# Chosen rows of an expert layer returned through DRAM, and layer 3's gate products moved to the end of an attention frame

## The chip, the cores and the metric

The kernel runs on one core of a Trainium2 chip. The metric is the device time of one execution in microseconds, as the median of several runs. The profile of one more execution shows where its time goes.

## The reference

The reference is a stack of eight sublayers on x of shape (8, 512, 128), each as `x = x + f(layernorm(x))`: four pairs of a token mixer and a feed-forward part. Three of them matter here.

```python
# layer 1's feed-forward part: 256 chosen rows get another value than the rest
x1 = einsum('btd,hd->bth', x, sw1) + sb1;  x2 = einsum('btd,hd->bth', x, sw2) + sb2
shared_out = einsum('bth,dh->btd', ln(silu(x1) * x2), sw3) + sb3
x_moe = x[index_b, index_t]                      # 256 rows
...                                              # gates, the best of 8 experts for each row
final_out = shared_out.at[index_b, index_t].set(shared_moe_out + expert_moe_out)

# layer 2's attention: 16 heads of 64 over 512 tokens, softmax over the query axis
scores = einsum('bhqp,bhkp->bhqk', q, k) / sqrt(64)
attn = softmax(scores, axis=2);  ctx = einsum('bhqk,bhkp->bqhp', attn, v)
out = concat(ctx) @ l_w.T + l_b

# layer 3's feed-forward part, with blockwise FP4 rounding of both sides
gate = fp4_linear(x, w_gate);  y = fp4_linear(x, w_up)     # 352 wide
out = fp4_linear(silu(gate) * y, w_down)
```

The indices are an input. In the data they name rows of the first two batches, but the kernel has to serve any.

## The kernel before

x lies in SBUF as eight blocks `x[b]` of 512 tokens (128 partitions, J = 4 tiles of 128). Every matmul is in float32; the profile counts each as two records. The order of instructions on every engine is the order in which the program calls them (`manual_schedule`), and each engine works its list in that order. Semaphore waits come from the tiles: a tile of a pool with n buffers waits until the tile n calls ago has been read.

Layer 0 and layer 1 come first. In layer 1, `stages` runs norms, linear attention and the shared part block by block; a written list of steps follows for the 256 chosen rows. `f_scale` writes each block's normed rows to the DRAM tile `by_rows` (SP's queue), `chosen_rows` gathers the 256 by two indirect transfers on GpSimd's queue (L968), and `chosen_out` leaves their new values in `val` (128 partitions, 2 rows each, 128 wide). `at_col` and `at_int` hold the rows' places, `rest` is 1 where a row is not chosen, and `inv` is one over how often it is.

To put `val` into x, the kernel makes a matrix `put` of zeros and ones for a block by comparing 0 to 511 with the places (`put_rows`, two DVE operations), multiplies it with `val` on TensorE (`put_product`: 8 matmuls, by way of `by_token`), and adds the product times `inv` (`scaled_add`, four DVE operations of L777). For block 0 this is at the end of layer 1 (`chosen_put`), before the norm of `x[0]`, its transposes and layer 2's first products. `keep_clock(n)` fills TensorE with products of the identity there. For blocks 1 to 7 it is in layer 2's frames 0 to 6 (`rows_in`).

`late` does layers 2 and 3 together. Layer 2's attention is cut into 64 frames n, one for a block and a pair of heads. A frame calls, in this order: `scores(n, 0)` (four products of q and k, the row maximum `nm` on DVE, four exponentials on ScalarE), with hook P between the exponentials of its two tiles; hook V; `context(n - 1)`; `weigh(n, 0)` (reciprocal on DVE, `vs` on GpSimd); hook G; `scores(n, 1)`; `queries(n + 2)` (q leaves PSUM by ScalarE, k by DVE); `output(n - 1)`; `values(n + 1)`; `weigh(n, 1)`; hook E. The steps of other layers are put into these hooks by `at(frame, hook, step)`. The PSUM banks are `two` (two buffers of two banks, for the scores), `c` and `o` (one each), and `one` with two buffers, which are given out in turn to queries (two), the gate products (two), each transpose and layer 3's convolution.

Layer 3 of block b follows by a plan of frames (`planned`), eight frames after that of the block before it: norm and a convolution of 20 taps (`conv_v` on DVE, `conv_s` on ScalarE and GpSimd, `conv_out` on TensorE), a second norm, FP4 rounding, four pairs of gate products `gated(j)` (two matmuls of 352 columns and a Tanh on ScalarE) with `gated_v(j)` on DVE, the rounding of h in two halves (`quant_h1`, `quant_h2`), its transposes (`turn_h(0)`, `turn_h(1)`) and the last product (`down`). Block 0's gate products are in frames 17 to 20, those of block 3 in frames 41 to 44, for example. Between frames 9 and 10 and between 17 and 18 layer 2's experts run for four blocks each.

Of the kernel before, what the change touches and what calls it, by code (L numbers as in the profile page):

```python
# [17 lines left out]
F32 = mybir.dt.float32  # L18
# [3 lines left out]
ALU = mybir.AluOpType  # L22
AX = mybir.AxisListType

P = 128
D = 128
NB = 8
TB = 512
# [132 lines left out]
def body(ctx, tc, dram, spans, x_in, ib, it, ic, ei, out):  # L161
# [527 lines left out]
    at_col = const.tile([P, 2], F32, tag="at_col", name="at_col")  # L689
    at_int = first.tile([P, 2], U32, tag="at_int", name="at_int")  # L690
    by_rows = tc.dram_tile([NT * P, D], F32, name="by_rows")
    inv = const.tile([P, NT], F32, tag="inv", name="inv")
    val = const.tile([P, 2, D], F32, tag="val", name="val")

# [78 lines left out]
    def scaled_add(b, pv, by):  # L773

        for j in range(J):
            t = b * J + j
            nc.vector.scalar_tensor_tensor(  # L777
                x[b][:, j, :], pv[:, j, :], by[:, t : t + 1], x[b][:, j, :], ALU.mult, ALU.add
            )

    def layer1():

# [5 lines left out]
        with tc.tile_pool(name="l1", bufs=2) as wp, tc.tile_pool(name="l1c", bufs=1) as once:  # L790
# [126 lines left out]
            def z_stats(b):  # L917
                t[b]["zby"] = stats_of(t[b]["z"], J)
# [178 lines left out]
            def chosen_out():  # L1097
# [25 lines left out]
                    val, val, po[:, : 2 * D].rearrange("p (m d) -> p m d", m=2), ALU.add  # L1123
                )

            def chosen_put():
                scaled_add(0, put_product(c_["put"]), inv)

# [22 lines left out]
            with tc.manual_schedule():  # L1151

                nc.scalar.activation(
                    stat.tile([P, J], F32, tag="nb", name="nb")[:, :1], half[:, :1], AF.Exp
                )
                for zt in zts:
                    nc.gpsimd.memset(zt[64:65, :], 1.0)
                for i in range(NB):
                    for f, lag in stages:
                        if 0 <= i + lag < NB and (f, i) != (turn_, 0):  # L1160
                            f(i + lag)


                gather(7)
                f_stats(5)
                output(6)
                z_scale(1)
                attend(7)
                f_scale(5)
                f_stats(6)  # L1170
                f_gate(2)
                turn_o(7)
                z_turn(1)
                output(7)
                f_stats(7)
                f_scale(6)
                chosen_biases()
                f_scale(7)
                z_out(1)
                z_stats(2)  # L1180
                chosen_rows()
                f_turn(5)
                f_gate(3)
                f_turn(6)
                z_stats(3)
                z_scale(2)
                f_gate(4)
                z_turn(2)
                f_turn(7)
                z_stats(4)  # L1190
                f_gate(5)
                z_out(2)
                z_stats(5)
                chosen_products()
                chosen_gates()
                z_scale(3)
                z_turn(3)
                chosen_select(0)
                f_product(6)
                z_out_by_three(3)  # L1200
                z_scale(4)
                z_turn(4)
                chosen_select(1)
                chosen_shared()
                chosen_norm()
                keep_clock(5)
                chosen_scale()
                z_out_by_three(4)
                t[6]["gated"]()
                z_stats(6)  # L1210
                f_product(7)
                chosen_mix()
                chosen_affine()
                keep_clock(8)
                chosen_turn()
                t[7]["gated"]()
                z_scale(5)
                c_["put"] = put_rows(0, wp, nc.vector)
                z_turn(5)
                chosen_out()  # L1220
                z_stats(7)
                z_scale(6)
                z_out_by_three(5)
                chosen_put()

                by = stats_of(x[0], J)
                z_turn(6)
                z_out_by_three(6)
                keep_clock(10)
                xn = norm.tile([P, J, D], F32, tag="xn", name="xn")  # L1230
                scaled(xn, x[0], by, J)
                nc.gpsimd.tensor_tensor(
                    x[0], x[0], bc["lb"].unsqueeze(1).to_broadcast([P, J, D]), ALU.add
                )
                keep_clock(6)
                t[0]["next"] = turned(norm, "xt", xn)
                z_scale(7)
                z_turn(7)
                z_out_by_three(7)
# [111 lines left out]
    def late():  # L1351
# [11 lines left out]
        with tc.tile_pool(name="a2", bufs=2) as wp, tc.tile_pool(name="l3", bufs=1) as lp:  # L1363
# [283 lines left out]
            def layer3(b, xp, tile_, part=(0, J), conv_bank="one", h_tag="h"):  # L1647
# [171 lines left out]
                stats2, scale2, _, t2 = norm_steps(b, None, None, part)  # L1819
                return SimpleNamespace(**{k: v for k, v in locals().items() if callable(v)})  # L1820

            def planned(b, f0_):

                s = layer3(b, *shared3(b))


                soon = b < 2 or b == NB - 2
                z = 9 - soon
                plan = [
                    (1, "V", s.stats) if b < 2 else (0, "E", s.stats),  # L1830
                    (1, "G", s.scale),
                    (1, "E", s.turn_),
                    (2, "V", lambda: s.conv_v(1, 2, 3, 4)),
                    (2, "G", lambda: s.conv_s(6, 7)),
                    (2, "E", lambda: s.conv_s(8, 9, 10)),
                    (2, "E", lambda: s.conv_v(5)),
                    (3, "G", lambda: s.conv_s(11, 12)),
                    (3, "E", lambda: s.conv_s(13, 14, 15)),
                    (4, "G", lambda: s.conv_s(16, 17)),
                    (4, "E", lambda: s.conv_s(18, 19, 20)),  # L1840
                    (5, "V", s.join),
                    (5, "E", s.conv_out),
                    (5, "E", s.stats2),
                    (6, "G", s.scale2),
                    (6, "E", s.quant_x1) if soon else (7, "V", s.quant_x1),
                    (z - 1, "V", s.quant_x2),
                    (z - 1, "E", s.turn_x),
                    (z + 2, "V", lambda: s.quant_h1(0)),
                    (z + 3, "V", lambda: s.quant_h2(0)),
                    (z + 4, "V", lambda: s.quant_h1(1)),  # L1850
                    (z + 5, "V", lambda: s.quant_h2(1)),
                    (z + 5, "P", lambda: s.turn_h(0)),
                    (z + 6, "P", lambda: s.turn_h(1)),
                    (z + 6, "E", s.down),
                ]
                for j in range(J):
                    plan.append((z + j, "P", lambda j=j: s.gated(j)))
                    plan.append((z + j, "V", lambda j=j: s.gated_v(j)))
                for frame, kind, f in plan:
                    at(f0_ + frame, kind, f)  # L1860
                return s
# [101 lines left out]
            def rows_in(b):  # L1963
                made = {}

                def make():
                    made["put"] = put_rows(b, lp, nc.vector, "cg")

                def product():
                    scaled_add(b, put_product(made["put"]), inv)  # L1970

                return make, product

            for b in range(1, NB):
                make, product = rows_in(b)
                at(b - 1, "V", make)
                at(b - 1, "E", product)

            with tc.manual_schedule():
                nc.vector.tensor_scalar(qb, a2["qb"], 0.125, None, ALU.mult)  # L1980
                fetch(0)
                xts[0] = t[0]["next"]
                queries(0)
                for n in range(N):
                    scores(n, 0, lambda: (n > 0 or (values(0), queries(1)), hook(n, "P")))
                    if n - 1 in experts_after:
                        waiting()
                    hook(n, "V")
                    if n - 1 in exs:
                        ct = context(n - 1)  # L1990
                    weigh(n, 0)
                    hook(n, "G")
                    scores(n, 1, lambda: None)
                    queries(n + 2)
                    if n > 0:
                        output(n - 1, ct)
                    values(n + 1)
                    weigh(n, 1)
                    hook(n, "E")
                    if n in experts_after:  # L2000
                        eb, made = experts_after[n]
                        kept = []
                        waiting = experts(eb, made["xt"], lambda: kept.append(context(n)))
                        ct = kept[0]
                end()
# [40 lines left out]
```

## Time and profile before

| | |
|---|---|
| median of 6 runs | 1521.85 us (1518.63 to 1525.66) |
| the profiled execution | 1515.39 us |
| its span | 1513.6 us, 22428 instructions |
| mean granted TensorE clock | 0.978 |
| frames 0 to 63 | begin at 552.81 us and 1428.92 us |
| exponentials of layer 2 | 512, 688 ns each (L1483) |
| products of the chosen rows | 128 records, 275 ns each (ps<-val,put) |
| DMA | 55.12 MB, mean 36 GB/s |

A profile line of the timeline gives the start in us from the span's start, the time from the first start to the last end of the group, then engine, line, operation, the tiles (out<-in), the shapes and the count; in brackets is the idle time before it and what ended it. Matmuls overlap in the records, so that a row of 16 of 275 ns takes less than 16 times that.

### The profile page before, as it was taken

To read this page: it belongs to the slowest core of one execution; us is meant where nothing else is said; L and a number is where in the kernel's file an instruction comes from. 1 tells how busy PE (TensorE), PEld (TensorE's weight loads), DVE (VectorE), ACT (ScalarE), POOL (GpSimd) and SP (SyncE) were. 2 spreads that over 40 slices of the span, in tenths; PEclk is the share of its full clock that TensorE was granted. 3 is DMA by queue.
4 is the path that set the end of the run, shared out by engine and by line. 5 is a ranking of instruction groups with operands and counts; after the bars stand their busy time and mean duration, and the time that the engine had idled before them with its cause. 6 is when DMAs were issued, how large, how long until landed. Compare 5 with 4: busy or idle time off the path is not lost.

```text
span 1513.6 us, 22428 instructions
## 1 busy us (share of the span) xinstructions
PE 1416.1 (94%) x7782; PEld 680.2 (45%) x7782; DVE 1031.7 (68%) x2129; ACT 1046.5 (69%) x2141; POOL 643.2 (42%) x742
## 2 busy tenths in 40 slices
PE   7789999998789889999999999999999999999975
PEld 3652222222366655543444444445445454454453
DVE  6776667767476636661664397786886877867857
ACT  6869999888776545564776486776776767767632
POOL 6647666665655321110441053352441623524432
PEclk9899999999999889999999999999999999999997
DMA  5049999977321010000100000000000000000000
GB/s 181 1 58 130 134 130 127 127 114 103 84 85 36 11 29 1 0 1 0 28 1 1 1 1 7 1 1 8 1 1 8 1 8 1 0 8 1 1 8 14
DMA packets 25443, 55.12 MB, mean 36 GB/s; under 512 B 5266, under 2 KB 18130, under 8 KB 20851
## 3 DMA queue, kind: packets, MB, share of 16 engines
q1 hardware_dynamic: 24688, 51.99, 20.4%
q10 hardware_dynamic: 578, 1.57, 0.3%
q8 instruction: 62, 1.02, 0.3%
q14 instruction: 51, 0.41, 0.1%
q0 software_dynamic: 64, 0.13, 0.0%
HBM read 47.35 MB, written 6.32 MB: 35 GB/s over the span
## 4 chain that ended last, share of the span: by engine, by line
PE 67%; ACT 13%; DVE 12%; DMA 4%; issue 2%; POOL 2%; SPq 0%; POOLq 0%; DVEq 0%; ACTq 0%
PE ps L247 65%; ACT hm L556 5%; DMA gs<-gates 3%; ACT ex L1483 2%; ACT hm L555 2%; DVE pr L568 1%; DVE nm L1477 1%; DMA gates<-eq 1%; POOL rs L244 1%; ACT xn L1399 1%; DVE fm L1284 1%; DVE s L702 1%; DVE frc L1267 1%; ACT xn L713 0%; DVE fa L1285 0%
## 5 line engine op out<-in xcount | busy, mean ns | idle before, releaser
L1483 ACT ACTIVATE ex<-ps,nm 128x512 f32<-128x512 f32 x512 | 345.8, 688 | 192.5 <-DVE nm L1477 192.5
L1477 DVE TENSOR_REDUCE nm<-ps 128x2 f32<-128x1024 f32 x256 | 300.4, 1215 | 48.3 <-PE ps L247 48.0
L247 PE MATMUL ps<-q,k 64*128 64x512 f32 x1024 | 258.4, 621 | 4.8 <-ACT ex L1483 4.0
L247 PE MATMUL ps<-ex,vs 128*64 128x512 f32 x1024 | 233.8, 598 | 0.0
L1498 POOL TENSOR_TENSOR vs<-v,sm 128x256 f32<-128x256 f32 x128 | 81.5, 637 | 337.5 <-DVE sm L1497 290.0
L574 POOL TENSOR_TENSOR acc<-acc,pr 128x512 f32<-128x512 f32 x119 | 166.6, 1400 | 107.6 <-DVE pr L568 102.9
L556 ACT ACTIVATE hm<-ps,blob_f 128x1536 f32<-128x1536 f32 x128 | 196.3, 1533 | 0.0
L247 PE MATMUL ps<-xt,blob_a 128*128 128x512 f32 x304 | 153.0, 630 | 0.1
L247 PE MATMUL ps<-h,w 32*128 32x512 f32 x1024 | 148.0, 639 | 3.6 <-DVE eq L467 1.9
L247 PE MATMUL ps<-hm,w 128*32 128x512 f32 x1024 | 136.4, 605 | 11.3 <-DVE pr L568 10.3
L247 PEld LDWEIGHTS ps<-q,k 64*128 64x128 f32 x1024 | 87.5, 186 | 131.1 <-issue 75.3
L568 DVE SCALAR_TENSOR_TENSOR pr<-ps,blob_f,gs 128x512 f32<-128x512 f32 x120 | 89.9, 749 | 74.5 <-PE ps L247 60.7
L1683 POOL TENSOR_TENSOR acs<-acs,prod 128x512 f32<-128x512 f32 (+1 forms) x104 | 130.0, 1250 | 14.3 <-ACT prod L1682 9.6
L247 PEld LDWEIGHTS ps<-ex,vs 128*64 128x64 f32 x1024 | 67.8, 136 | 144.5 <-issue 124.3
L243 POOL TENSOR_SCALAR rs<-mv 128x4 f32<-128x4 f32 (+1 forms) x69 | 17.7, 257 | 213.0 <-DVE mv L1389 146.4
L555 ACT ACTIVATE hm<-ps,blob_f 128x512 f32<-128x512 f32 x128 | 88.0, 687 | 29.0 <-PE ps L247 28.9
L1483 ACT ACTIVATION_READ_ACCUMULATOR ex<-ps,nm 128x1 f32 x512 | 105.6, 206 | 0.0
L247 PEld LDWEIGHTS ps<-xt,blob_a 128*128 128x128 f32 x304 | 53.2, 194 | 87.8 <-issue 60.5
L1445 DVE TENSOR_TENSOR v<-ps,blob_bc 128x512 f32<-128x512 f32 x64 | 44.2, 691 | 70.7 <-PE ps L247 44.2
L247 PEld LDWEIGHTS ps<-h,w 32*128 32x128 f32 x1024 | 40.9, 183 | 111.7 <-ACT hm L555 86.1
L247 PEld LDWEIGHTS ps<-blob_a,ct 128*128 128x128 f32 x512 | 67.0, 191 | 32.3 <-issue 29.2
L244 POOL TENSOR_TENSOR rs<-rs,half 128x4 f32<-128x4 f32 (+1 forms) x69 | 72.4, 1050 | 5.8
(292 smaller groups left out, 2265.6 us busy)
## 6 DMA issues: line engine op xcount, KB each, us to landing
gs<-gates SPq DMA_DIRECT2D x256, 128.0 KB
blob_f<-in_f SPq DMA_DIRECT2D x1, 2560.0 KB
blob_a<-in_a SPq DMA_DIRECT2D x1, 2056.0 KB
x<-in_x SPq DMA_DIRECT2D x8, 256.0 KB
gates<-eq SPq DMA_DIRECT2D x8, 256.0 KB
by_rows<-fxn SPq DMA_DIRECT2D x8, 256.0 KB
ge<-gates SPq DMA_DIRECT2D x4, 512.0 KB
out<-x SPq DMA_DIRECT2D x7, 256.0 KB
```

What stands on the lines that cost most here:

```text
L243: nc.gpsimd.tensor_scalar(t, var, EPS, None, ALU.add)
L244: nc.gpsimd.tensor_tensor(t, t, half[:, : t.shape[-1]], ALU.pow)
L247: nc.tensor.matmul(out_, lhs, rhs, start=start, stop=stop)
L555: nc.scalar.activation(hm[:, 0, :], p1, AF.Gelu, bias=bias)
L556: nc.scalar.activation(hm[:, 1:, :], p3, AF.Gelu, bias=bias)
L568: nc.vector.scalar_tensor_tensor(pr, po, f0["b2"][:, e : e + 1], gs, ALU.add, ALU.mult)
L574: nc.gpsimd.tensor_tensor(acc[:, b, :], acc[:, b, :], pr, ALU.add)
L1445: nc.vector.tensor_tensor(v, pv, bias, ALU.add)
L1477: nc.vector.tensor_reduce(nm, ps, AX.X, ALU.max, negate=True)
L1483: nc.scalar.activation(ex[kt][:, i, :], ps[:, i, :], AF.Exp, bias=nm[:, i : i + 1], accum_out=sm[:, kt, i : i + 1],)
L1498: nc.gpsimd.tensor_tensor(vs[:, tiles, :, :], vs_[n][:, tiles, :].rearrange("p j (i n) -> p j i n", i=2), sm[:, tiles, :].unsqueeze(3).to_ ...
L1683: nc.gpsimd.tensor_tensor(t["acs"], t["acs"], p, ALU.add)
```

## The change

It has two parts. The rows of blocks 1 to 7 no longer come by a product. At the start of layer 1, a cleared tile `nought` is written by SP's queue to blocks 1 to 7 of a new DRAM tile `back`. After `chosen_out`, `chosen_back` scatters `val` to its places in `back` by two indirect transfers on GpSimd's queue. In frames 0 to 6, hook V issues a read of one block of `back` on SP's queue into a tile "cg", and hook E adds it to `x[b]` on GpSimd. Block 0 stays with its product.

In layer 3, the gate products j = 1 to 3 of blocks 1 and up go from hook P of frame z + j to hook E of the same frame, behind `values(n + 1)`, and their `gated_v` goes from hook V of that frame to hook V of the next. In those frames (`early_q`) `queries(n + 2)` is called between the exponentials of `scores(n, 1)`, where it stood behind them. `turn_h(0)` goes from hook P to hook E of frame z + 5, for all blocks of the plan. z is 8 for blocks 0, 1 and 6 and 9 otherwise, counted from the block's first frame (9 for block 0, 17 for block 1, then 24, 32 and so on).

```diff
+    back = tc.dram_tile([NT * P, D], F32, name="back")
...
+            def chosen_back():
+                for m in range(2):
+                    nc.gpsimd.indirect_dma_start(
+                        back, bass.IndirectOffsetOnAxis(at_int[:, m : m + 1], 0), val[:, m, :], None
+                    )
...
                 for zt in zts:
                     nc.gpsimd.memset(zt[64:65, :], 1.0)
+                nought = once.tile([P, J, D], F32, tag="nought", name="nought")
+                nc.gpsimd.memset(nought, 0.0)
+                for b in range(1, NB):
+                    nc.sync.dma_start(
+                        back[b * TB : (b + 1) * TB, :].rearrange("(j p) d -> p j d", p=P), nought
+                    )
...
                 chosen_out()
+                chosen_back()
                 z_stats(7)
...
+            early_q = set()
...
+                for j in range(J):
+                    if b > 0 and j > 0:
+                        early_q.add(f0_ + z + j)
+                        plan.append((z + j, "E", lambda j=j: s.gated(j)))
+                        plan.append((z + j + 1, "V", lambda j=j: s.gated_v(j)))
+                    else:
+                        plan.append((z + j, "P", lambda j=j: s.gated(j)))
+                        plan.append((z + j, "V", lambda j=j: s.gated_v(j)))
...
-                    (z + 5, "P", lambda: s.turn_h(0)),
+                    (z + 5, "E", lambda: s.turn_h(0)),
                     (z + 6, "P", lambda: s.turn_h(1)),
                     (z + 6, "E", s.down),
-                for j in range(J):
-                    plan.append((z + j, "P", lambda j=j: s.gated(j)))
-                    plan.append((z + j, "V", lambda j=j: s.gated_v(j)))
...
-                def make():
-                    made["put"] = put_rows(b, lp, nc.vector, "cg")
-                def product():
-                    scaled_add(b, put_product(made["put"]), inv)
+                def fetch_rows():
+                    made["rows"] = lp.tile([P, 4, TB], F32, tag="cg", name="rows")[:, 0, :]
+                    nc.sync.dma_start(
+                        made["rows"].rearrange("p (j d) -> p j d", j=J),
+                        back[b * TB : (b + 1) * TB, :].rearrange("(j p) d -> p j d", p=P),
+                    )
+                def add():
+                    rows_ = made["rows"].rearrange("p (j d) -> p j d", j=J)
+                    nc.gpsimd.tensor_tensor(x[b], x[b], rows_, ALU.add)
...
-                    scores(n, 1, lambda: None)
-                    queries(n + 2)
+                    scores(n, 1, lambda: queries(n + 2) if n in early_q else None)
+                    if n not in early_q:
+                        queries(n + 2)
```

More of the change, by code (lines that the diff above doesn't have):

```diff
@@ L1847, in planned @@
                     (z - 1, "E", s.turn_x),
+                ]
+                for j in range(J):
[6 more added lines that the diff above has]
+                        plan.append((z + j, "V", lambda j=j: s.gated_v(j)))
+                plan += [
                     (z + 2, "V", lambda: s.quant_h1(0)),
@@ L1964, in rows_in @@
                 made = {}
-                def make():
-                    made["put"] = put_rows(b, lp, nc.vector, "cg")
-                def product():
-                    scaled_add(b, put_product(made["put"]), inv)
-                return make, product
+                def fetch_rows():
[7 more added lines that the diff above has]
+                    nc.gpsimd.tensor_tensor(x[b], x[b], rows_, ALU.add)
+                return fetch_rows, add
             for b in range(1, NB):
-                make, product = rows_in(b)
-                at(b - 1, "V", make)
-                at(b - 1, "E", product)
+                fetch_rows, add = rows_in(b)
+                at(b - 1, "V", fetch_rows)
+                at(b - 1, "E", add)
             with tc.manual_schedule():
```

## The prediction

> **What bounds the kernel now.** I read the page first: the busy line and the chain that ended last.
>
> ```profile
> PE 1416.1 (94%) x7782; PEld 680.2 (45%) x7782; DVE 1031.7 (68%) x2129; ACT 1046.5 (69%) x2141; POOL 643.2 (42%) x742
> ...
> PE 67%; ACT 13%; DVE 12%; DMA 4%; issue 2%; POOL 2%; SPq 0%; POOLq 0%; DVEq 0%; ACTq 0%
> ```
>
> TensorE is both the busiest engine and two thirds of the chain, so I asked for the stage that the diff touches, cut into frames. A frame runs from one frame's first score product (ps<-q,k) to the next. The columns are the stretch, its length, and busy time of PE, PEld, DVE, ACT and POOL, then the clock and DMA.
>
> ```profile
> 632.12:645.03 12.91, 12.91 (x70) 6.85 (x69) 9.31 (x23) 6.73 (x18) 2.70 (x5) 1.00 0.00 0
> 656.58:667.70 11.12, 11.12 (x53) 5.06 (x53) 6.75 (x9) 7.13 (x19) 1.23 (x2) 1.00 0.00 0
> ...
> 1189.82:1202.32 12.50, 12.50 (x58) 5.73 (x57) 11.41 (x14) 9.20 (x23) 8.92 (x8) 1.00 0.00 0
> ...
> 1215.22:1227.14 11.92, 11.92 (x59) 5.66 (x58) 11.24 (x29) 7.76 (x24) 6.31 (x8) 1.00 0.00 1
> ```
>
> These are frames 6, 8, 44 and 46. PE is busy for the whole of each. A bare frame (8) is 11.12 us; frame 6 adds one product of chosen rows, 44 one pair of gate products (1.38 us), 46 six transposes of h (0.80). So a frame is as long as its PE work, and two things follow. Work taken off PE shortens a frame by its full length; work moved inside a frame gains nothing, and loses if it must wait in the new place.
>
> **The rows: what leaves.** In frames 0 to 6 eight products (16 records) go from PE, and six DVE operations with them. The PE timeline of frame 4 ends so:
>
> ```profile
> 617.34 1.95 PE L247 MATMUL ps<-val,put 128*128 128x128 f32 x16
> 619.22 1.99 PE L247 MATMUL ps<-q,k 64*128 64x512 f32 x8
> ```
>
> From 617.34 to 619.22 is 1.88 with the 0.1 that any frame has at its end, so the product is worth 1.78 us, and 12.90 - 11.12 = 1.78 says the same. Nothing is late next: frames 8 and 13 are such frames without it and have no idle PE. In frame 0 the last exponential of the frame ends 12.70 us in, and the second score product of frame 1 asks for its bank at 13.4. Sum: 7 x 1.78 = 12.46 us off. The DVE operations (2 x 0.48 and 4 x 0.34 per block) were beside PE work and count as nothing.
>
> **The rows: what comes.** Per block one SP read of 256 KB and one POOL add of 128x512, 1.27 us by the row of L954. The add stands behind vs of its frame (ends about 12.8 us in), and the next vs that queues behind it is due at 5.6 in the frame after; the read is issued when the previous add frees its tile, about 3 us into the frame, and the indirect reads of before landed in 2.7 us. That leaves some 6 us; without that cover, vs and the context product behind it would be late by what is missing. I take 0.
>
> In layer 1, POOL clears one tile behind three clears of 0.52 us, before the first rs. SP's seven writes stand before by_rows, which is first issued 27 us later: 0. POOL's q and v operations follow, and PE waits for the v clear at 416.11, so I take 0.3 us; the bounds are 0 and 0.5.
>
> At the end of layer 1 the two scatters stand on POOL between val and the rs of z_stats(7). Their price is that of the two gathers, one engine and size (other direction, so between nothing and twice):
>
> ```profile
> 501.18 1.23 POOL L968 DMA_INDIRECT row<-by_rows,at_int  x1 [2.21 <-DMA by_rows<-fxn]
> 502.71 0.96 POOL L968 DMA_INDIRECT row<-by_rows,at_int  x1 [0.30 <-DVE s L898]
> ...
> 503.70 0.26 POOL L243 TENSOR_SCALAR rs<-mv 128x4 f32<-128x4 f32 x1
> ```
>
> The wait before the first ended at 500.35, so POOL is held 3.35 us. val is done at 534.48: POOL is free at 537.85 where the rs of z_stats(7) now starts at 535.37. Behind it queue that norm's three operations (1.65 us), the add to x[5] (1.27) and the rs, power and nb of x[0] (1.65), which end at 542.5, not 540.86. ACT's xn waits for that nb:
>
> ```profile
> 540.89 1.65 ACT L713 ACTIVATE xn<-x,nb,rs 128x128 f32<-128x128 f32 x4 [0.29 <-POOL nb L707]
> 543.41 0.58 ACT L737 COPY xt<-ps 128x512 f32<-128x512 f32 x1 [0.87 <-PE ps L735]
> ```
>
> Of the 1.65 a part is hidden: keep_clock's products held PE until 542.77, after xn was ready (542.54). Now the last xn ends at 544.2, the transposes follow, and the copy starts at 544.57: 1.16 us late, and zn, zt, zo, the last x and queries(0) with it, since each waits for the one before. Bounds 0 (scatter free) and 4.5 (twice the time). I take 1.16.
>
> **Layer 3: what moves.** Fifteen pairs of gate products (blocks 1 to 5, j 1 to 3) go from P to E of their frame. They need the two banks that queries holds; in those frames queries is put between the exponentials, so q ends before the last two. 0 gained (no idle PE), and 0 lost if k and q are out by 11.02 us, where the values product ends. Frame 44 decides, for its hook holds most DVE work:
>
> ```profile
> 1192.14 1.21 DVE L1477 TENSOR_REDUCE nm<-ps 128x2 f32<-128x1024 f32 x1
> 1193.27 1.16 DVE L1281 TENSOR_SCALAR fm<-fa 128x704 int32<-128x704 int32 x1
> 1194.46 1.48 DVE L1284 TENSOR_SCALAR fm<-fm 128x704 f32<-128x704 f32 x1
> ```
>
> Beside POOL's three adds (1191.42 to 1195.56) fm took 1.16 and 1.48; in frame 46 without them 0.54 and 0.53. Afterwards gated_v (1.08) comes first, from 3.45 to 4.53 us in the frame; the adds, 1.27 each from 0.95, are over at 4.8; the four operations take 2.96 as in frame 46, to 7.8; nm twice 2.32, k 0.7: k ends at 10.8. Frame 45 gets a gated_v more than before: 3.45 + 1.08 + 2.5 for the scale + 0.7 join, and k ends at 10.7. Both clear 11.02, by 0.2 and 0.3. The Trainium skill ("SBUF — State Buffer", section "SBUF: two separate sides") says that GpSimd and a DVE operation of two SBUF inputs or a two-port mode lock each other out for whole instructions. Those rows agree; by that rule, too, gated_v, which reads one operand from PSUM, would not be held.
>
> The first transposes of h, turn_h(0), go from P to E, in frames where queries is not early. They use the same two banks: the first waits for k, the second for q, which is ACT's last work of the frame. Frame 46, on DVE, PE and ACT:
>
> ```profile
> 1226.04 0.74 DVE L1456 TENSOR_SCALAR k<-ps,blob_a 128x512 f32<-128x512 f32 x1
> ...
> 1226.16 1.06 PE L247 MATMUL ps<-blob_a,xt 128*128 128x128 f32 x8
> ...
> 1227.69 0.70 ACT L1455 ACTIVATE q<-ps,qb 128x512 f32<-128x512 f32 x1
> ```
>
> k ends 11.56 and q 13.17 us into the frame. Neither gets earlier: both follow nm, which follows the hook's DVE work (its last, L1286, ends 8.57 in), not PE. PE, free at 11.02, waits to 11.6, does three transposes (0.40), waits to 13.2, does three, and the next frame starts at 13.71 where it was 11.92: 1.79 us lost. So in frames 30, 38, 46, 54: 7.16. In frame 22 (block 0) the convolution's output stands behind it and takes the bank that ACT's two ht copies (0.53) must clear after q (ends 13.64): products from 14.2, 1.98 us of them, end 16.18 instead of 14.07: 2.11. Frame 62 has no queries left, its scores wait for exponentials anyway, and ht leaves ACT ahead of them: 0.2 gained.
>
> **The sum**, against the profiled execution's 1515.39 us (span 1513.6 and 1.79 around it): -12.46 + 0.3 + 1.16 + 7.16 + 2.11 - 0.2 = -1.93, so 1513.46. The median of the runs is 1521.85, 6.46 above this execution; I carry the difference over: 1519.9. 0.2% is 3 us, about what a measurement of this kernel can tell from no change.
>
> **Rivals.** *Slower: k late.* If the port is held as it is now, frame 44's hook ends at 9.0 as before, k at 12.02, and the gate products wait 1.05; in frame 45 the scale costs 3.09 as now, k ends at 11.3 and the convolution waits 0.35. Five blocks: 7.0, so +5.1, 1527.0. It decides from 11.02 on. For it: margins of 0.2 and 0.3; against: the adds start earlier than now.
>
> *Faster: the transposes do not wait* (q out early, or the banks free). Then 9.27 of loss goes: -11.2, 1510.7. Against it: frames 22, 30, 38, 46 and 54 are not among those with early queries.
>
> *The slow clock lasts.* PEclk is 0.52 from 546 to 553, 0.50 to 556 and 0.94 from 556 to 560. A later start may find this stretch a piece of 4 us longer or shorter, at half speed 2 us either way: 1518 to 1522. The Trainium skill ("TensorE: Matmul & The Clock Gate", "Part 1: The HAM clock gate") has full rate return only after a busy window of about 3.4 us that runs free of the kernel; as an estimate by that page, 1.7 either way. The trace's half-rate stretch does not contradict it.
>
> *The rows do not come in time.* Then vs would wait on POOL in frames 0 to 6; above 6 us of lateness only. Small.
>
> **How the numbers follow.** Forecast 0.55, with its own range 1516.7 to 1523.2 (a scatter that delays by 0 to 4.5 us gives 1518.7 to 1523.2, and the clock may take 2 more off); k late 0.20; no wait 0.13; clock longer 0.07; rows late 0.05. A quarter of the forecast's share lies beyond 3 us on the fast side, when scatter, clear or clock cost less; with the no-wait rival and some of the clock this gives faster 0.29. Slower is the k rival and late rows, less what falls inside 3 us: 0.22. The rest, 0.49, is the same. The range takes in the forecast and the k rival: 1515.5 to 1527.5.
>
> **What would show it.** Frames 1, 2, 3, 5, 6 at 11.12 us without idle PE (else the first term is wrong). DMA_INDIRECT twice after val and xt's copy about 1.2 us later behind val. Frames 42 to 45 as long as before; a stall before ps<-wt_gate in 44 or ps<-blob_l,xp in 45 is the slower rival. In 30, 38, 46, 54 two stalls before transposes of h, of 0.55 and 1.2 us, released by k and q, and a frame of 13.7; frames of 11.9 there would make the prediction wrong by 7 us.

## The result, and the profile after

The changed kernel takes 1512.65 us as the median of 38 runs (1507.86 to 1521.35). The kernel before takes 1518.76 us as the median of 80 runs (1510.44 to 1526.42). The ratio is 0.9964, 95% interval 0.9954 to 0.9975: a gain of 5.5 us (3.8 to 7.0), more than the 3 us that a measurement can tell from no change. The prediction had a gain of 1.93 us on top of a median of 1521.85, hence 1519.9, with the most weight on "no difference". The profiled execution after took 1514.04 us, its span is 1512.2 us.

The page after, its busy line and its chain:

```profile
PE 1407.3 (93%) x7670; PEld 671.2 (44%) x7670; DVE 1002.8 (66%) x2087; ACT 1050.2 (69%) x2141; POOL 648.7 (43%) x752
...
PE 66%; ACT 14%; DVE 13%; DMA 3%; POOL 2%; issue 2%; SPq 0%; POOLq 0%; DVEq 0%; ACTq 0%
```

TensorE has 112 records fewer (the seven blocks' products) and is busy for 8.8 us less, and it is still what bounds. The frames tell more. Frames 6, 44, 46 and 54 after, in the columns of the prediction (length, then PE, PEld, DVE, ACT, POOL, clock, DMA):

```profile
625.35:636.47 11.12, 11.12 (x54) 5.06 (x53) 7.55 (x17) 6.74 (x19) 3.86 (x6) 1.00 0.09 25
...
1185.92:1198.22 12.30, 12.30 (x57) 5.66 (x56) 10.04 (x14) 9.97 (x24) 8.74 (x8) 1.00 0.01 2
1211.13:1224.82 13.69, 12.20 (x59) 5.64 (x58) 12.01 (x31) 8.57 (x24) 6.92 (x9) 1.00 0.01 2
1314.17:1326.59 12.42, 11.99 (x60) 5.62 (x59) 10.77 (x22) 8.56 (x24) 3.70 (x6) 1.00 0.00 1
```

Frame 6 is now a bare frame. Frame 44, with gate products at E, is 12.30 where it was 12.50, and PE is busy throughout both times: this is the surprise. Frame 46 is 13.69 with 1.49 of idle PE, where the prediction had 13.7, and frame 54 only 12.42. Frame by frame, in us after less before at full clock:

| place | measured | prediction's step |
|---|---|---|
| rows' products, frames 0 to 6 | -12.50 | -12.46 |
| clear of `nought`, layer 1 | +0.25 | +0.3 |
| last copy of xt behind val, layer 1 | +1.57 | +1.16 |
| frames 19 to 21 (block 0's gates) | +0.61 | 0 |
| frame 22 (transposes of h, block 0) | +2.01 | +2.11 |
| frames 30, 38, 46 | +5.33 | +5.37 |
| frame 54 | +0.50 | +1.79 |
| the fifteen frames with gate products at E | -2.92 | 0 |
| frame 62 | -0.37 | -0.2 |
| sum | -5.52 | -1.93 |

The clear is read from the rows alone (below), whose half-clock stretches there lie within 0.12 us of those of the kernel before: from the first clear of `zt` to the clear of `v` it is 6.50 us against 6.25, and counted from there the third to sixth copies of xt in layer 1 are later by the same 0.25, the end of val by 0.17. In frame 0 only 1.78 of the difference is the product's; the rest of its 3.58 is the clock, which was back before frame 0 in this execution and 3.7 us into it in the kernel before. The sum agrees with the measured 5.5. What does not enter it is where the two executions had TensorE at half clock: frame 0 begins at 558.55 us against 552.81, yet four profiles of kernels that are alike up to that point (before, and the gates alone, transposes alone and gates at G below) have it at 552.81, 562.02, 554.38 and 563.87. So a span difference of 5 us between two profiles is not evidence here; frames, and offsets from one instruction to the next at the same clock, are.

### The profile page after: what moved, and what is told of

It is laid out like the page before. It is cut to its first block, busy times and chain, and to the rows that moved or that the text cites. A ratio compares the mean times of both kernels' runs of the same rounds, so it can differ in the third digit from the quotient of the medians.

```text
span 1512.2 us, 22178 instructions
## 1 busy us (share of the span) xinstructions
PE 1407.3 (93%) x7670; PEld 671.2 (44%) x7670; DVE 1002.8 (66%) x2087; ACT 1050.2 (69%) x2141; POOL 648.7 (43%) x752
## 3 DMA queue, kind: packets, MB, share of 16 engines
q10 hardware_dynamic: 578, 1.57, 0.3%
## 4 chain that ended last, share of the span: by engine, by line
PE 66%; ACT 14%; DVE 13%; DMA 3%; POOL 2%; issue 2%; SPq 0%; POOLq 0%; DVEq 0%; ACTq 0%
PE ps L247 63%; ACT hm L556 5%; ACT ex L1498 3%; ACT hm L555 2%; DVE nm L1492 2%; DMA gs<-gates 2%; DVE pr L568 1%; DVE s L1402 1%; POOL rs L244 1%; DVE fm L1299 1%; DVE fa L1300 1%; DVE fa L1301 1%; DVE s L703 1%; ACT xn L714 1%; DMA gates<-eq 1%
## 5 line engine op out<-in xcount | busy, mean ns | idle before, releaser
L247 PE MATMUL ps<-hm,w 128*32 128x512 f32 x1024 | 136.4, 605 | 11.1 <-DVE pr L568 10.3
```

The lines of the kernel that those rows point to most:

```text
L247: nc.tensor.matmul(out_, lhs, rhs, start=start, stop=stop)
```

## Experiments

All were timed in five rounds beside the kernel before. Times from rounds carry some 3 us of uncertainty; frames repeat within 0.02 us from profile to profile, so the frames decide where they can.

### The parts by themselves

**Rows alone**: the changed kernel with layer 3's plan and `queries` as before.

```diff
-                        plan.append((z + j, "E", lambda j=j: s.gated(j)))
-                        plan.append((z + j + 1, "V", lambda j=j: s.gated_v(j)))
+                        plan.append((z + j, "P", lambda j=j: s.gated(j)))
+                        plan.append((z + j, "V", lambda j=j: s.gated_v(j)))
-                    (z + 5, "E", lambda: s.turn_h(0)),
+                    (z + 5, "P", lambda: s.turn_h(0)),
```

> Layer 3's order is that of the kernel before; only the rows of blocks 1 to 7 go through DRAM. Both theories have 7 x 1.78 = 12.46 us leave frames 0 to 6. The prediction's own steps add 0.3 for the clear and 1.16 for the scatters: -11.0 us against the kernel before. If the rows are what brought the extra gain (nothing lost at the end of layer 1), -12.5; if the later start of frame 0 seen in the changed kernel's profile (558.55 against 552.81 us, 5.7 later, 1.8 of it given back in frame 0) is a real cost of the scatters and not the slow clock of one execution, -8 to -9.

Measured: 1509.94 us, ratio 0.9943 (0.9922 to 0.9963), -8.7 us (5.6 to 11.8). Frames 1 to 62 together are 851.09 against 861.75, 10.66 less, six times 1.78. With frame 0's product, the 1.57 of the copy and the 0.25 of the clear that makes -10.6, inside the interval.

**Gates alone**: the kernel before with the plan's gate part and `early_q` of the change, and nothing else.

> Only the fifteen pairs of gate products (and the early queries of their frames) move; rows and first transposes of h as in the kernel before. The prediction's term is 0. The theory read from the two traces: each of the fifteen frames gets 0.20 us shorter (12.50 to 12.30), because TensorE changes the form of its matmuls fewer times, so -3.0 us. The rival of the prediction (k late) would be +5.

Measured: 1516.82 us, ratio 0.9984 (0.9961 to 1.0006). The rounds can't tell -3 from 0, the frames can: all fifteen are 12.30, and frame 19 is 13.57. Frames 1 to 62 are 2.26 shorter.

**Transposes alone**: the kernel before with one word changed.

```diff
-                    (z + 5, "P", lambda: s.turn_h(0)),
+                    (z + 5, "E", lambda: s.turn_h(0)),
```

> Only the first transposes of h move from hook P to hook E of their frame. The prediction's terms: 4 x 1.79 + 2.11 - 0.2 = +9.1 us. Read from the two traces: +2.0 in frame 22, 1.78 in each of 30, 38 and 46, but 0.5 in 54 and -0.4 in 62, so +7.5. The rival that the transposes do not wait: 0.

Measured: 1529.45 us, ratio 1.0078 (1.0056 to 1.0101), +11.8 us (8.5 to 15.3): more than any theory had. Frames 22, 30, 38, 46, 54 and 62 are those of the changed kernel (+7.5), but frame 31 took 16.68 instead of 15.04: TensorE's clock was at half for 3.41 us right behind frame 30's stall. The clocks of all the runs point the same way. The span times the granted clock is an estimate of the time at full clock, and the rest of the span is what half clock cost. The mean of the first is 1486.9 us in the twelve runs and 1480.5 in those of the kernel before beside them, 6.4 more; that of the second is 41.8 against 36.4, 5.4 more. The last section comes back to it.

**Without the transposes** (named e4_no_turn in a later expectation): the changed kernel with `turn_h(0)` at P.

> The changed kernel with the first transposes of h back in hook P. If the three parts add up as the traces say (-11 for the rows, -3 for the gate products, +7.5 for the transposes), this is 7 to 8 us faster than the changed kernel and -13 to -14 us against the kernel before, about 1505. By the prediction's steps (gate products at 0, transposes +9.1) -11 against before and -9.1 against the changed kernel. If the transposes do not matter, the same as the changed kernel, -5.5.

Measured: 1506.17 us, ratio 0.9914 (0.9884 to 0.9944), -13.1 us. Frames 1 to 62 are 848.75, 7.5 less than in the changed kernel. The parts add up: rows and gates gain, the transposes take over half of it back.

### Why the transposes wait

**Early queries in their frames too**, so that k and above all q leave the two banks sooner:

```diff
+                early_q.add(f0_ + z + 5)
```

> The changed kernel, with queries also called early in the frames of the first transposes of h, so that k and q leave their banks 1.6 us sooner. Theory (the transposes wait for k and q): the stalls go, frame 22 from 16.09 back to about 13.9, frames 30, 38 and 46 from 13.70 to 11.72 (11.92 less 0.2 for one change of matmul form fewer), 54 from 12.42 to 11.72: -8.8 us against the changed kernel, -14 against the kernel before. If the cost lies in the place itself (transposes of h beside the products of output and values) and not in k and q, these frames stay at 13.70 and the time is that of the changed kernel.

Measured: 1507.07 us, ratio 0.9925 (0.9897 to 0.9953). The stall for q goes, that for k stays: frames 30, 38, 46 are 12.42 instead of 13.70, frame 54 is 11.77, frame 22 still 16.08. Frames 1 to 62 are 4.5 shorter than in the changed kernel, half of what was expected. TensorE in the changed kernel's frame 46, then in frames 22 and 30 of this one:

```profile
1222.74 0.55 PE L1805 MATMUL ps<-blob_c,h 128*128 128x128 f32 x3 [0.42 <-DVE k L1471]
1224.35 0.55 PE L1805 MATMUL ps<-blob_c,h 128*128 128x128 f32 x3 [1.06 <-ACT q L1470]
```

```profile
912.23 0.87 PE L1805 MATMUL ps<-blob_c,h 128*128 128x128 f32 x6 [0.90 <-DVE k L1471]
914.25 1.16 PE L247 MATMUL ps<-blob_l,xp 128*128 128x128 f32 x8 [1.14 <-ACT ht L1811]
...
1019.34 0.88 PE L1805 MATMUL ps<-blob_c,h 128*128 128x128 f32 x6 [0.42 <-DVE k L1471]
```

The brackets name the two waits that the prediction had: k, then q. With q early all six transposes run together (x6), but k still follows nm, which follows the hook's DVE work, so calling queries early does not move it. In frame 22 the wait for q has only changed its name: the two ht copies now stand behind the frame's last exponentials on ScalarE, and the convolution waits for them about as long as before (1.14 us, 1.06 in the changed kernel). My expectation had overlooked both. ScalarE of this frame:

```profile
913.00 0.70 ACT L1498 ACTIVATE ex<-ps,nm 128x512 f32<-128x512 f32 x1
...
914.07 0.40 ACT L1808 COPY ht<-ps 128x256 f32<-128x256 f32 x1
914.33 0.30 ACT L1811 COPY ht<-ps 96x128 f32<-96x128 f32 x1
```

### Where the gate products' 0.2 us comes from

**Gates at hook G** in the kernel before, between the values product and the second scores:

```diff
                 for j in range(J):
-                    plan.append((z + j, "P", lambda j=j: s.gated(j)))
-                    plan.append((z + j, "V", lambda j=j: s.gated_v(j)))
+                    kinds = "GG" if b > 0 and j > 0 else "PV"
+                    plan.append((z + j, kinds[0], lambda j=j: s.gated(j)))
+                    plan.append((z + j, kinds[1], lambda j=j: s.gated_v(j)))
```

> The kernel before with the same fifteen pairs of gate products at hook G, between the values product and the second pair of scores, with their DVE part right behind. TensorE then changes the form of its matmuls five times a frame, as in the kernel before (scores, values, gates, scores, queries), where the changed kernel has four. Theory of the forms: frames 26 to 28 and their like stay at 12.50 us, the time is that of the kernel before. Rival (the gain comes from leaving hook P, or from standing behind the values product): 12.30 in those frames, -3 us. If the DVE part at G makes the second row maxima late: over 12.50, slower.

Measured: 1518.1 us, ratio 0.9987 (0.9962 to 1.0012); the fifteen frames are 12.50. So neither leaving P nor standing behind the values product gains anything. TensorE's timeline of frame 44 in the kernel before, in this one and in the changed one (start, length, then operation; "64*128" or "128*128" is the part of the array that the weights fill):

```profile
1191.74 0.86 PE L247 MATMUL ps<-wt_gate,xt 128*128 128x352 f32 x2
1192.43 0.76 PE L247 MATMUL ps<-wt_up,xt 128*128 128x352 f32 x2
1193.12 3.65 PE L247 MATMUL ps<-ex,vs 128*64 128x512 f32 x16
```

```profile
1204.59 0.86 PE L247 MATMUL ps<-wt_gate,xt 128*128 128x352 f32 x2
1205.29 0.76 PE L247 MATMUL ps<-wt_up,xt 128*128 128x352 f32 x2
1205.97 1.99 PE L247 MATMUL ps<-q,k 64*128 64x512 f32 x8
```

```profile
1196.05 1.06 PE L247 MATMUL ps<-blob_a,xt 128*128 128x128 f32 x8
1196.94 0.76 PE L247 MATMUL ps<-wt_gate,xt 128*128 128x352 f32 x2
1197.54 0.75 PE L247 MATMUL ps<-wt_up,xt 128*128 128x352 f32 x2
1198.22 0.70 PE L247 MATMUL ps<-q,k 64*128 64x512 f32 x2
```

From the first gate product to the second it is 0.69 and 0.70 us at P and G, 0.60 at E, although the two are alike in all three. The first product behind a change of the array's form takes 0.1 more, and so does the last ahead of one. Record by record, the two of wt_gate start 0.400 us apart at P and G, behind a change, and 0.299 at E. The two of wt_up, with no change beside them, start 0.296 apart, and from the second of them to a product of another form it is 0.389. At E the gate products follow products of their own form, so one of five changes a frame goes: 0.2. The Trainium skill ("TensorEngine Tiling (Array Packing)", section "Key Properties") says that changing the tiling mode, and not just the tile, drains TensorE; it gives no time. The traces agree that a change costs time, and give 0.2 us for one.

### The scatters, and what can be had

**Late scatters**: `chosen_back()` behind the norm of `x[0]`, its transposes and its add.

```diff
                 chosen_out()
-                chosen_back()
...
                 t[0]["next"] = turned(norm, "xt", xn)
+                chosen_back()
                 z_scale(7)
```

> The changed kernel with the two scatters behind the norm of x[0] and its add on GpSimd, instead of behind val. Theory (the scatters hold GpSimd 3.0 us ahead of rs): from val's end to the copy of xt 8.93 us as in the kernel before, where it is 10.50 in the changed kernel; -1.5 us. If something else moved that copy, 10.50 and the same time as the changed kernel.

Measured: 1515.77 us, ratio 0.9976 (0.9950 to 1.0001), against an expected 1511. The mechanism is as expected: the copy of xt stands 8.93 us behind val's end, 10.49 in the changed kernel. GpSimd and ScalarE in the changed kernel, where val ends at 538.54, then ScalarE in this one, where it ends at 538.94:

```profile
538.83 1.11 POOL L1130 DMA_INDIRECT back<-val,at_int  x1 [7.12 <-DVE s L703]
541.48 0.96 POOL L1130 DMA_INDIRECT back<-val,at_int  x1 [1.54 <-DMA back<-val,at_int]
542.46 0.26 POOL L243 TENSOR_SCALAR rs<-mv 128x4 f32<-128x4 f32 x1
```

```profile
549.03 0.59 ACT L738 COPY xt<-ps 128x512 f32<-128x512 f32 x1 [0.42 <-PE ps L736]
```

```profile
547.87 0.58 ACT L738 COPY xt<-ps 128x512 f32<-128x512 f32 x1 [0.87 <-PE ps L736]
```

The time did not follow. The profiled execution, too, lost clock behind stalls. Four stretches of it: frame 22 up to the loss, the loss, frame 38, and frame 39 (the column before the last two is the clock):

```profile
895.23:909.79 14.56, 12.59 (x63) 6.11 (x63) 12.28 (x24) 9.41 (x26) 10.12 (x10) 1.00 0.00 0
909.79:913.20 3.41, 3.41 (x17) 3.15 (x17) 0.43 (x1) 0.26 (x2) 0.00 (x0) 0.50 0.02 5
1107.17:1120.87 13.70, 12.22 (x59) 5.65 (x59) 12.02 (x31) 8.56 (x24) 6.92 (x9) 1.00 0.01 2
1120.87:1137.55 16.68, 16.68 (x88) 9.41 (x87) 8.23 (x12) 10.24 (x29) 2.83 (x4) 0.90 0.00 0
```

Frame 22 took 17.43 (+1.34) and frame 39 took 16.68 (+1.64). Over its twelve runs half clock cost 42.4 us, in the changed kernel's 38.6, and at full clock its runs are 1.8 us shorter (1471.4 against 1473.2, estimates as above). Why these runs lost more is not shown. That the scatters' place is worth some 1.5 us is shown by offsets, not by this kernel's rounds. The offset carries on to frame 0: from val's end to its first score product it is 20.01 us in the changed kernel and 18.32 in the best version below, both with 6.83 us of half clock in between.

**Three repairs at once**: early queries as above, late scatters, and block 0's `gated_v` and `quant_h1` in the old order.

> The changed kernel with early queries in the frames of the first transposes, the scatters behind the norm of x[0], and block 0's gated_v and quant_h1 in the order of the kernel before (frame 19 back from 13.57 to 12.97). If the three add up: -8.8 - 1.5 - 0.6 = -10.9 us against the changed kernel, about -16.5 against the kernel before, 1502 us. If only the early queries count: -8.8 against the changed kernel.

Measured: 1507.4 us, ratio 0.9926 (0.9901 to 0.9951), -11.2 us. Frame 19 is 12.97 again; the frames of the transposes are as with early queries alone, for the same reasons.

**The best version**: instead of early queries, the transposes back at P; late scatters and block 0's old order.

> The changed kernel with the first transposes of h back in hook P, the two scatters behind the norm of x[0], and block 0's gated_v and quant_h1 in the order of the kernel before. Added up from the frames: rows -12.5, gate products -3.0, no stall, frames 19 to 21 as before, and the copy of xt 8.93 us after val: -15.5 us against the kernel before, 1503, and 2.1 us faster than the kernel of e4_no_turn. If the place of the scatters makes no difference to the end, only 0.6 faster than that one.

Measured: 1501.63 us, ratio 0.9900 (0.9868 to 0.9932), -15.2 us (10.3 to 20.0): faster than both kernels. Frames 1 to 62 are 848.16, against 848.75 without the transposes. In the same rounds the kernel without the transposes and the changed kernel ran once more:

> The kernel of e4_no_turn once more, beside the best version and the changed kernel on one chip. By the frames -13.4 us against the kernel before and -7.9 against the changed kernel; the first six runs gave -12.0 and -6.5.

Measured: 1504.01 us, ratio 0.9915 (0.9889 to 0.9941), as the first time. The best version is 2.4 us faster in these rounds, less than they can tell; its frames and the offset to frame 0 add up to 2.3.

> The changed kernel once more, for a second profile of it and a comparison on this chip. By the frames and the copy of xt -5.5 to -6 us against the kernel before. In the profiles of the kernel with the transposes alone and of the one with late scatters, TensorE's clock fell to half for 3.41 us right behind a stall before the transposes of h (frames 31, 22 and 39), 1.4 to 1.6 us lost each time; in the first profile of the changed kernel it did not. If that comes with the stalls in some executions, this profile or its runs may hold one or two of them; in kernels without these stalls it has not been seen between frames 10 and 62.

Measured: 1514.24 us, ratio 0.9977 (0.9951 to 1.0003), in line with the 0.9964 of all its runs. Its frames repeat the first profile to 0.02 us, with no loss of clock in them.

## Why the prediction was wrong

**Right.** The rows' term is right to 0.04 us, and nothing was late next: frames 1, 2, 3, 5 and 6 are 11.12. The stalls of the first transposes came in the frames, at the places and with the releasers that the prediction named, and cost 1.78 each in frames 30, 38 and 46 and 2.01 in frame 22. The rival of the late k did not happen: k ends 10.50 us into frame 44 and 10.71 into frame 45, before 11.02. `gated_v` took 0.51 and 0.52 beside GpSimd's adds (until 1190.63) and was not held. The Trainium skill ("SBUF — State Buffer", section "SBUF: two separate sides") has the lock only for VectorE operations with two SBUF inputs or in a two-port mode; `gated_v` reads one operand from PSUM, and the trace agrees. The rows arrived in time. GpSimd and VectorE of frames 44 and 45 after:

```profile
1186.65 3.98 POOL L1698 TENSOR_TENSOR acs<-acs,prod 128x512 f32<-128x512 f32 x3 [0.27 <-ACT prod L1697]
1189.37 0.51 DVE L1773 SCALAR_TENSOR_TENSOR s<-s,ps 128x352 f32<-128x352 f32 x1
1189.91 0.52 DVE L1774 SCALAR_TENSOR_TENSOR h<-s,ps 128x352 f32<-128x352 f32 x1
1195.68 0.74 DVE L1471 TENSOR_SCALAR k<-ps,blob_a 128x512 f32<-128x512 f32 x1
...
1208.19 0.74 DVE L1471 TENSOR_SCALAR k<-ps,blob_a 128x512 f32<-128x512 f32 x1
```

The rival "the transposes do not wait" gives nearly the measured time (1510.7), but that is luck: its mechanism is refuted by frames 30, 38 and 46, and the gain has other sources.

**The step that failed: "0 gained (no idle PE)"** for the moved gate products. It rests on "work moved inside a frame gains nothing", and that holds only as long as the work costs the same in both places. It cost 0.2 us less in each of fifteen frames, -2.92 in all, because one change of the array's form goes. The trace of before showed it: the two records of wt_gate, behind the change, start 0.400 us apart, those of wt_up, which are as long, 0.296. The prediction gave the changes of form no price.

**Mis-sized: the fourth stall**, "1.79 us lost ... in frames 30, 38, 46, 54". I read frame 46 and counted four. Frame 54 of the kernel before, which was there to be read, ends its k and q earlier:

```profile
1326.83 0.74 DVE L1456 TENSOR_SCALAR k<-ps,blob_a 128x512 f32<-128x512 f32 x1
```

```profile
1328.64 0.71 ACT L1455 ACTIVATE q<-ps,qb 128x512 f32<-128x512 f32 x1
```

From its start at 1317.07 that is 10.5 and 12.28 us, not 11.56 and 13.17; a product that is ready at 11.02 never waits for k. In frame 46 VectorE works on two sets of norm statistics ahead of k, in frame 54 on one; the second set takes 1.25 us of frame 46 and ends so:

```profile
1220.36 0.36 DVE L1389 BATCH_NORM_AGGREGATE mv<-s 128x2 f32<-128x6 f32 x4
1220.76 0.17 DVE L1391 TENSOR_SCALAR nb<-mv 128x4 f32<-128x4 f32 x1
```

The loss in frame 54 is 0.50, 1.29 less. Frame 62 gave 0.17 more than taken.

**Missed: block 0's order**, +0.61. Its products stay at P, but the rewritten plan calls `gated_v(2)` ahead of `quant_h1(0)` in frame 19, where it stood behind. DVE of the kernel before and after:

```profile
871.98 0.88 DVE L1265 TENSOR_REDUCE fsc<-h 128x44 f32<-128x704 f32 x1
```

```profile
864.32 0.52 DVE L1773 SCALAR_TENSOR_TENSOR s<-s,ps 128x352 f32<-128x352 f32 x1 [0.80 <-ACT s L1770]
```

Before, the reduction of a finished h filled the time in which Tanh was under way; after, DVE waits 0.80 us for Tanh and all behind it is late.

**The scatters** cost 1.57 at the copy against 1.16 (GpSimd is held 3.9 us from val to rs, not 3.35, since the second waits 1.54 us for the first to land; the second gather had waited 0.30). The clear cost 0.25, near the 0.3 that was taken.

**The level.** Of the 7.25 us between 1519.9 and 1512.65, 3.6 come from these terms. Another 3.1 come from the starting point, the step "I carry the difference over": the median of the six runs shown was 1521.85, that of 80 is 1518.76. Neither alone takes the time below the range's 1515.5; together they do. The last 0.6 is inside what the runs can tell. Executions of the kernel before spread over 16 us and more, and go with their mean clock (in the later rounds 1510.12 us at 0.981, 1526.15 at 0.969). The range took its bounds from the mechanisms and none from this; by the profiled execution alone (1515.39), 1513.46 would have been forecast, near the result by luck.

## What to carry to other kernels

A product that is moved on a full TensorE is not free of price or gain: count how often the form of the array changes in the old and in the new order, and read the change's price off the starts of two equal products. When a stall is counted once and multiplied, read each place, since the engines that release it need not be equally late everywhere. Before a step is moved into banks that another step still holds, compare the time at which those banks are released with the time at which TensorE would arrive, and after a plan is rewritten, compare the order in every hook, also of the blocks that it means to leave alone.

## What the runs showed of the hardware

One change of the array's form costs 0.2 us here, in two halves: 0.1 on the last product ahead of it (0.389 for 0.296 us from start to start) and 0.1 on the first behind it (0.400 for 0.299).

The half-clock stretches of an execution all begin on one grid of 3.413 us, whose position differs from execution to execution: in the late scatters they begin at 909.79 and 1121.42, 62 steps apart, in the transposes alone at 1029.39. Between frames 10 and 62 the clock fell three times in all profiles, each time behind a window of that grid that held both parts of a transposes' stall: TensorE idle for 1.48 us (transposes alone, frame 30), 1.97 and 1.48 (late scatters, frames 22 and 38), of 3.41. Thirteen other windows with 1.42 to 1.59 idle were followed by no loss, and three of them held both parts of such a stall too (frame 30 in both profiles of the changed kernel, frame 46 of the transposes alone). So if the idle time of a window decides, the bound is near 1.5 and not sharp, as the ends of matmuls in the records are modelled. The Trainium skill ("TensorE: Matmul & The Clock Gate", "Part 1: The HAM clock gate") has the clock fall after an idle window of about 3.4 us; here it fell behind windows that were still busy for 42 to 57%, and the measurement decides. So a stall of 1.8 us cost 1.3 to 1.6 more in some of the executions in which it fell into one window. That is the likely reason why the transposes alone measured 11.8 us where their frames add up to 7.5. Their runs lost 5.4 us more to half clock than the kernel before, but where in the runs without a profile they lost it was not seen.
